# Where the largest scores of a softmax round are split, turned and read back: an attention and feed-forward kernel on one Trainium2 core

## The chip, the cores and the metric

The kernel runs on one core of one Trainium2 chip. The metric is the device time of one execution in microseconds (us); lower is better. The kernel before was timed three times: 3776.87, 3777.06 and 3780.1 us, median 3777.06 us.

A core has five engines with an instruction queue each: TensorE (PE in the profile; PEld is its loading of weights), VectorE (DVE), ScalarE (ACT), GpSimd (POOL) and SyncE (SP), which in this kernel only issues DMAs. An engine takes its queue in order; semaphores hold an instruction until what it reads is written and what it overwrites has been read.

## The reference

`x` is 4096 tokens by 256. What is computed, cut to what matters:

```python
def attention(x):
    proj = quant4(x) @ ternary_weight(Wqkv_w).T + Wqkv_b
    q = proj.reshape(B, N, h, dk).transpose(0, 2, 1, 3)     # h = 16 heads, dk = 16
    k = v = proj.reshape(B, h, N, dk)
    q, k = rotary(q), rotary(k)
    att = einsum(q @ U, k @ U) / sqrt(dk)                   # 16 x 4096 x 4096
    return quant4(softmax(att) @ v) @ ternary_weight(Wo_w).T

x = layernorm(x + attention(x))
h = silu(tlin(x, w1, s1)) * tlin(x, w2, s2)                 # 256 -> 1024
h = gelu(tlin(h, h1, hs1)); h = gelu(tlin(h, h2, hs2))      # 1024 -> 1024
out = layernorm(x + tlin(h, w3, s3))                        # 1024 -> 256
```

The softmax needs the largest score of each of the 16 x 4096 rows before the exponentials. The feed-forward weights are whole numbers; the kernel tests that on the chip, since rounded weights give the same product only then.

## The kernel before

**Tiling.** The heads go in eight pairs, the queries in eight blocks of 512. One (pair, block) is a round `u`, so there are 64 rounds, and each has 32 steps; step `s = 32 u + i`. A step does two things for two different rounds:

- `largest(s)` for round `u`: two matmuls (one for each head of the pair, `ps`, L468) give 128 queries by 512 keys of scores in a PSUM bank each, and VectorE takes the largest of each row (`mx`, L476). The `ps` buffers come from a pool of three banks (`ps_1`), two are used by each step, and other short work (L361 to L400, L439, L553) takes a bank of the same pool.
- `weights(s - 40)` for the round before or the one before that (`LAG` is 40 steps): four matmuls (L511) put scores minus the row's largest score into `sc`, a pool of two buffers, so that `sc` of step `s` waits for the exponential of step `s - 2`; ScalarE takes the exponential (`pr`, L519). The first two of the four matmuls subtract the largest scores: they multiply a matrix of -1 by `m_rows`.

Every second step `values` (L533) multiplies eight blocks of exponentials with the values. An odd step issues `largest` first and then `weights`, an even step the other way round (L700 to L705). So TensorE's order over an odd and an even step is: scores for the largest of the odd step, `weights` of the odd step, `weights` of the even step, scores for the largest of the even step, values. In what follows such a pair of steps is called a period, and it is measured from the start of an odd step's L468 matmuls to the next odd step's. A round is 16 periods.

**The largest scores of a round.** At the end of `largest` of step 31, VectorE does four short instructions in a row: it joins the partial maxima (`m`, L481), rounds them to a high part (L485), takes the remainder as a low part (L486), and turns blocks of 32 x 32 (`m_turned`, L489). SyncE writes `m_turned` to DRAM (L494) and reads it back as four rows (L499, four DMAs of 16 pieces of 128 bytes): high and low part of both heads, 512 queries in a row. That is `m_rows`, first used at step 8 of the next round (40 steps after the round began).

**Test of the weights.** In the even rounds 8 to 50, at step 14, `check_weights` loads one of 22 pieces of weights (128 x 1024) through SyncE (L589), and GpSimd rounds it and takes the difference (L593, L594). At step 30, `largest_difference` lets VectorE reduce the absolute differences of the piece to one column of `differ` (L597). At step 0 of round 52 `set_flag` makes a flag from it, by which the feed-forward part is chosen.

**Other work in the rounds.** ScalarE copies finished values at step 11 (L548), turned queries at step 26 (L446) and, in the rounds 3 to 6, 11 to 14 and so on, pieces of the next pair's keys (L362, L376, L400); VectorE forms the low part of the keys (L377) after ScalarE's L376. At step 0 of the rounds 4, 12, 20 and so on the first L376 falls on the boundary between two rounds. GpSimd rotates the next queries (L329 to L334, L431, L432), from step 6 of each round.

**What sets the order.** The program is written out under a manual schedule: `at(step, f)` files `f` in `todo[step]`, and the loop at L696 runs the list of a step ahead of that step's `largest` and `weights`. Each engine gets its instructions in that order. Within a list, what was filed first is first.

After the 64 rounds the feed-forward part (L708 on) takes the last part of the span; the change does not touch it.

Of the kernel before, what the change touches and what calls it, by code (L numbers as in the profile page):

```python
# [9 lines left out]
F32 = mybir.dt.float32  # L10
# [3 lines left out]
AF = mybir.ActivationFunctionType  # L14
ALU = mybir.AluOpType
AX = mybir.AxisListType
PSUM = bass.MemoryType.PSUM

P = 128
# [7 lines left out]
NQB = N // QB  # L27
NKT = N // P
DH = 1024
NC = DH // P  # L30
BT = 4
# [6 lines left out]
def attn_ffn_kernel(  # L38
# [22 lines left out]
    nc = tc.nc  # L61
# [4 lines left out]
    stat = ctx.enter_context(tc.tile_pool(name="stat", bufs=4))  # L66
# [13 lines left out]
    dram = ctx.enter_context(tc.tile_pool(name="dram", bufs=1, space=bass.MemoryType.DRAM))  # L80
# [157 lines left out]
    with ExitStack() as actx:  # L238
# [16 lines left out]
        m_parts = big.tile([P, 2, 2, 2, BT], F32R, name="m_parts")  # L255
        m_turned = big.tile([P, 32], F32, name="m_turned")
        m_rows = [big.tile([P, QB], F32R, name=f"m_rows{i}") for i in range(2)]
        m_dram = [dram.tile([P, 32], F32, name=f"m_dram{i}") for i in range(2)]

        qpool = actx.enter_context(tc.tile_pool(name="qpool", bufs=2))  # L260
        ppool = actx.enter_context(tc.tile_pool(name="ppool", bufs=8))
# [194 lines left out]
        def at(step, f):  # L456
            todo.setdefault(step, []).append(f)

        def largest(s):

            u, i = divmod(s, NKT)
            qt, ck = divmod(i, NKT // BT)
            if i == 0:
                mxs[u] = stat.tile([P, BT, 2, NKT // BT], F32, name="mx")
            ps = [ps_1.tile([P, 512], F32, name="ps1") for j in range(2)]
            for j in range(2):
                rows = slice(64 * j, 64 * j + 64)
                nc.tensor.matmul(  # L468
                    ps[j],
                    lhsT=qTs[u][rows, ts(qt, P)],  # L470
                    rhs=kTs[u // NQB][rows, ts(ck, 512)],
                    start=True,
                    stop=True,
                )
            for j in range(2):
                nc.vector.tensor_reduce(  # L476
                    mxs[u][:, qt, j, ck : ck + 1], ps[j], AX.X, ALU.max
                )
            if i == NKT - 1:
                m = stat.tile([P, 2, BT], F32, name="m")  # L480
                nc.vector.tensor_reduce(  # L481
                    m, mxs.pop(u).rearrange("p t j c -> p j t c"), AX.X, ALU.max
                )
                parts = m_parts[:, 0]
                nc.vector.tensor_copy(parts[:, :, 0, :], m)  # L485
                nc.vector.tensor_tensor(  # L486
                    parts[:, :, 1, :], m, parts[:, :, 0, :].bitcast(F32), ALU.subtract
                )
                nc.vector.transpose(  # L489
                    m_turned, m_parts.bitcast(F32).rearrange("p a j k t -> p (a j k t)")  # L490
                )

                turned = m_dram[u % 2]
                nc.sync.dma_start(out=turned, in_=m_turned)  # L494
                turned = turned.rearrange("(b a j k t) c -> a j k t b c", b=4, a=2, j=2, k=2)
                for j in range(2):
                    for k in range(2):
                        row = m_rows[u % 2][64 * j + k : 64 * j + k + 1, :].bitcast(F32)
                        nc.sync.dma_start(  # L499
                            out=row.rearrange("o (t b c) -> o t b c", t=BT, b=4),  # L500
                            in_=turned[0, j, k].unsqueeze(0),
                        )

        def weights(s):

# [70 lines left out]
                in_=yu.rearrange("p t j e -> p t (j e)"),  # L576
            )

        differ = stat.tile([P, 32], F32, name="differ", bufs=1)
        nc.gpsimd.memset(differ, 0.0)  # L580

        chunks = [
# [10 lines left out]
            nc.gpsimd.tensor_copy(r, w)  # L593
            nc.gpsimd.tensor_tensor(w, w, r.bitcast(F32), ALU.subtract)  # L594

        def largest_difference(i):
            nc.vector.tensor_reduce(  # L597
                differ[:, i : i + 1], wchunks.pop(i), AX.X, ALU.max, apply_absolute_value=True
            )

        def set_flag():

# [8 lines left out]
        with tc.manual_schedule():  # L611
            wchunks = {}
            for i in range(len(chunks)):
                at(NKT * (NQB + 2 * i) + 14, lambda i=i: check_weights(i))
                at(NKT * (NQB + 2 * i) + 30, lambda i=i: largest_difference(i))
            at(NKT * (NQB + 2 * len(chunks)), set_flag)
            later = set_up()
            for f in projection_steps(0, nc.vector):
                f()
            kTs[0] = kpool.tile([P, N], F32R, name="kT")  # L620
            steps = key_steps(0, kTs[0], nc.vector)
            for f in steps[:8]:
                f()
            for i, f in enumerate(steps[8:]):
                at(max(i - 1, 0), f)
            at(NQB, later)
            for b in range(1, NQB):
                steps = projection_steps(b, nc.gpsimd)
                first = NKT * (b - 2) + 16 if b > 1 else 0
                if b > 1:  # L630
                    at(
                        max(first - 20, 0),
                        lambda b=b: nc.sync.dma_start(out=x_bufs[b % 2], in_=x_t[:, ts(b, BT), :]),
                    )
                for f, step in zip(steps, (1, 1, 11, 14, 16) if b > 1 else (0, 0, 10, 13, 15)):
                    at(first + step, f)

            def load_scales():
                for name, src in (("s1", s1), ("s2", s2), ("hs1", hs1), ("hs2", hs2), ("s3", s3)):
                    nc.sync.dma_start(out=scales[name], in_=src)  # L640

            at(NKT * NQB, load_scales)
            for u in range(NU):
                pair, qb = divmod(u, NQB)
                if qb == 2 and pair + 1 < H // 2:
                    def start_keys(pair=pair, u=u):
                        kTs[pair + 1] = kpool.tile([P, N], F32R, name="kT")
                        steps = key_steps(pair + 1, kTs[pair + 1])
                        for i, f in enumerate(steps):
                            at(NKT * u + 40 + 6 * i, f)  # L650
                    at(NKT * u + 8, start_keys)

                def start_queries(u=u, pair=pair, qb=qb):
                    qTs[u] = qpool.tile([P, QB], F32R, name="qT", bufs=3)
                    natural, transposed = query_steps(pair, qb, qTs[u])
                    natural()
                    at(NKT * (u - 1) + 26 if u else 0, transposed)

                if u:
                    at(NKT * (u - 1) + (18 if u == 1 else 6), start_queries)  # L660
                else:
                    start_queries()
                base = NKT * u + LAG
                for kt in range(0, NKT, 2):
                    at(base + kt + 1 + AVLAG, lambda s=NKT * u + kt: values(s))
                at(base + NKT + AVLAG - 1, lambda u=u: finish(u, 0))
                at(base + NKT + AVLAG + 3, lambda u=u: finish(u, 1))
            last = NKT * NU
            at(last - 240, lambda: load_weights(w1_sb, w1T, 0))
            w2_sb, h1_sb, h2_sb = [None, None], [None, None], [None, None]  # L670

            def load_w2(k):
                w2_sb[k] = kprep.tile([P, 1, DH], F32R, name=f"w2_{k}", tag=("kr", "krT")[k])
                load_weights(w2_sb[k], w2T, k)

            for k in range(2):
                at(last - 230 + 10 * k, lambda k=k: load_w2(k))

            def load_h1(i):
                if i:  # L680
                    h1_sb[1] = kprep.tile([P, NC // 2, DH], F32R, name="h1b", tag="kn")
                else:
                    h1_sb[0] = kpool.tile([P, NC // 2, DH], F32R, name="h1a", tag="kT")
                load_weights(h1_sb[i], h1T, i * NC // 2)

            for i in range(2):
                at(last - 180 + 40 * i, lambda i=i: load_h1(i))
                at(last - 90, lambda i=i: load_x(i))

            def start_front():  # L690
                steps = front_steps(0, lambda shape, dt: ps_1.tile(shape, dt, name="ps1"))
                for i, f in zip((0, 6, 10, 12, 16, 18, 20), steps):
                    at(last + 2 + i, f)

            at(last - 60, start_front)
            for s in range(NKT * NU + LAG + AVLAG + 6):  # L696
                while todo.get(s):
                    todo[s].pop(0)()

                if s < NKT * NU and s % 2:  # L700
                    largest(s)
                if 0 <= s - LAG < NKT * NU:
                    weights(s - LAG)
                if s < NKT * NU and not s % 2:
                    largest(s)  # L705
# [213 lines left out]
```

## Time and profile before

| | us |
|---|---|
| median of three timed runs | 3777.06 |
| the profiled execution, its own time | 3776.26 |
| its span in the profile | 3774.5 |
| TensorE busy, of the span | 3693.2 |
| VectorE busy | 3081.1 |
| ScalarE busy | 2351.2 |
| GpSimd busy | 458.9 |
| weight loads of TensorE that waited for VectorE's `mx` (L476), 956 times | 707.3 |
| ScalarE waiting for TensorE's `sc` (L511) ahead of the exponential, 1032 times | 900.0 |
| TensorE's loads for `sc` waiting for ScalarE's exponential, 32 times | 22.8 |

The page gives the busy time of each engine, the chain of work that ended last, and groups of instructions by line with the mean time of one and what ended the idle time ahead of them. The timeline gives instructions in order of time, neighbours of one kind merged: start, duration of the whole group, engine, line, output and input, and how many; a bracket holds the idle time ahead of it and what ended it. A busy TensorE is not a TensorE at its peak, since the ends of matmuls are modelled. Times in the timeline count from the start of the span.

### The profile page before, as it was taken

To read this page: it belongs to the slowest core of one execution; us is meant where nothing else is said; L and a number is where in the kernel's file an instruction comes from. 1 tells how busy PE (TensorE), PEld (TensorE's weight loads), DVE (VectorE), ACT (ScalarE), POOL (GpSimd) and SP (SyncE) were. 2 spreads that over 40 slices of the span, in tenths; PEclk is the share of its full clock that TensorE was granted. 3 is DMA by queue.
4 is the path that set the end of the run, shared out by engine and by line. 5 is a ranking of instruction groups with operands and counts; after the bars stand their busy time and mean duration, and the time that the engine had idled before them with its cause. 6 is when DMAs were issued, how large, how long until landed. Compare 5 with 4: busy or idle time off the path is not lost.

```text
span 3774.5 us, 61722 instructions
## 1 busy us (share of the span) xinstructions
PE 3693.2 (98%) x24651; PEld 2084.5 (55%) x24651; DVE 3081.1 (82%) x5404; ACT 2351.2 (62%) x2630; POOL 458.9 (12%) x776
## 2 busy tenths in 40 slices
PE   6999999999999999999999999999999999999998
PEld 3444545555555555545455555555555548888887
DVE  6988998899889988998899889988999945555544
ACT  1566767776776767767766776767777773333333
POOL 3342011002101110011001100110010000000000
PEclk6999999999999999999999999999999999999999
DMA  1000000000000000000000000000010020000000
GB/s 36 13 14 3 9 9 9 9 9 9 9 9 9 9 9 9 9 9 9 9 9 9 8 9 9 9 3 25 3 47 14 9 70 6 17 17 23 28 6 12
DMA packets 83448, 50.92 MB, mean 13 GB/s; under 512 B 58320, under 2 KB 78032, under 8 KB 83152
## 3 DMA queue, kind: packets, MB, share of 16 engines
q1 hardware_dynamic: 79328, 35.36, 3.6%
q0 software_dynamic: 3824, 11.54, 0.9%
q8 instruction: 195, 3.19, 0.4%
q14 instruction: 101, 0.83, 0.1%
HBM read 37.44 MB, written 9.44 MB: 12 GB/s over the span
## 4 chain that ended last, share of the span: by engine, by line
PE 89%; DVE 10%; issue 1%; ACT 0%; POOL 0%; DMA 0%; SPq 0%; ACTq 0%; DVEq 0%
PE av L533 25%; PE sc L511 22%; PE ps L468 20%; PE ps_mm L751 17%; DVE mx L476 7%; PE ps L553 1%; PE ps L393 1%; PE ps L439 1%; DVE differ L597 1%; PE ps L367 0%; DVE m L481 0%; DVE m_turned L489 0%; DVE m_parts L485 0%; DVE m_parts L486 0%; PE ps L361 0%
## 5 line engine op out<-in xcount | busy, mean ns | idle before, releaser
L476 DVE TENSOR_REDUCE mx<-ps 128x1 f32<-128x512 f32 x4096 | 2552.0, 683 | 279.6 <-PE ps L468 261.0
L519 ACT ACTIVATE pr<-sc 128x1024 f32<-128x1024 f32 x2048 | 2004.2, 1023 | 902.0 <-PE sc L511 900.0
L468 PEld LDWEIGHTS ps<-kT,qT 64*128 64x128 f32 x4096 | 574.0, 185 | 1020.2 <-DVE mx L476 707.3
L468 PE MATMUL ps<-kT,qT 64*128 64x512 f32 x4096 | 1101.2, 471 | 27.4 <-DVE mx L476 23.1
L533 PE MATMUL av<-pr,v_all 128*32 128x512 f32 x8192 | 1091.4, 605 | 0.0
L511 PE MATMUL sc<-m_rows,minus 64*128 64x512 f32 x4096 | 865.0, 403 | 3.1 <-ACT pr L519 3.0
L511 PE MATMUL sc<-qT,kT 64*128 64x512 f32 x4096 | 836.1, 390 | 0.0
L511 PEld LDWEIGHTS sc<-qT,kT 64*128 64x128 f32 x4096 | 418.6, 185 | 80.2
L511 PEld LDWEIGHTS sc<-m_rows,minus 64*128 64x128 f32 x4096 | 412.3, 185 | 75.8 <-ACT pr L519 22.8
L533 PEld LDWEIGHTS av<-pr,v_all 128*32 128x32 f32 x8192 | 161.6, 108 | 258.6 <-issue 257.5
L784 ACT ACTIVATE gate<-ps_mm,sc_hs 128x512 f32<-128x512 f32 x128 | 88.2, 689 | 312.6 <-PE ps_mm L751 269.5
L733 DVE CAST h<-gate 128x512 fp32r<-128x512 f32 x128 | 54.4, 425 | 223.0 <-ACT gate L784 223.0
L593 POOL CAST wround<-xs 128x1024 fp32r<-128x1024 f32 x22 | 22.8, 1038 | 1115.5 <-DMA xs<-in_h1T 394.9
L735 DVE TENSOR_TENSOR h<-gate,h 128x512 fp32r<-128x512 f32 x192 | 132.4, 689 | 5.1
L751 PE MATMUL ps_mm<-h,h1a 128*128 128x512 f32 x512 | 128.9, 394 | 0.0
L751 PE MATMUL ps_mm<-h,h2a 128*128 128x512 f32 x512 | 127.1, 390 | 0.0
L751 PE MATMUL ps_mm<-h,h2b 128*128 128x512 f32 x512 | 126.5, 389 | 0.0
L751 PE MATMUL ps_mm<-h,h1b 128*128 128x512 f32 x512 | 126.5, 389 | 0.0
L431 POOL CAST qq<-qn 128x256 fp32r<-128x256 f32 x64 | 25.5, 398 | 739.2 <-PE ps L439 737.1
L776 DVE SCALAR_TENSOR_TENSOR gate<-ps_mm,sc_s,gate 128x512 f32<-128x512 f32 x64 | 48.0, 751 | 81.9 <-ACT gate L774 58.0
L751 PEld LDWEIGHTS ps_mm<-h,h1b 128*128 128x128 f32 x512 | 96.1, 188 | 20.1
L751 PEld LDWEIGHTS ps_mm<-h,h2b 128*128 128x128 f32 x512 | 96.1, 188 | 20.0
(147 smaller groups left out, 1963.7 us busy)
## 6 DMA issues: line engine op xcount, KB each, us to landing
xs<-in_x SPq DMA_DIRECT2D x16, 512.0 KB
m_rows<-m_dram SPq DMA_DIRECT2D x256, 2.0 KB
y_dram<-yu SPq DMA_DIRECT2D x64, 64.0 KB
xs<-in_h1T SPq DMA_DIRECT2D x8, 512.0 KB
xs<-in_h2T SPq DMA_DIRECT2D x8, 512.0 KB
yb<-y_dram SPq DMA_DIRECT2D x8, 512.0 KB
out<-xs SPq DMA_DIRECT2D x8, 512.0 KB
h1a<-in_h1T POOLq DMA_DIRECT2D x2, 1024.0 KB, 6.2
```

The costliest lines, as they stand in the source:

```text
L393: nc.tensor.matmul(ps[:, ts(k, P)], lhsT=flat[:, ts(4 * i + k, P)], rhs=identr, start=True, stop=True,)
L439: nc.tensor.matmul(ps[:, ts(t, P)], lhsT=qq[:, t].rearrange("p j k e -> p (j k e)"), rhs=identr, start=True, stop=True,)
L468: nc.tensor.matmul(ps[j], lhsT=qTs[u][rows, ts(qt, P)], rhs=kTs[u // NQB][rows, ts(ck, 512)], start=True, stop=True,)
L476: nc.vector.tensor_reduce(mxs[u][:, qt, j, ck : ck + 1], ps[j], AX.X, ALU.max)
L511: nc.tensor.matmul(ps[:, j, :], lhsT=minus[rows, :] if first else kTs[u // NQB][rows, ts(kt, P)], rhs=m_rows[u % 2][rows, :] if first else ...
L519: nc.scalar.activation(pr, ps, AF.Exp)
L533: nc.tensor.matmul(avs[u][strip : strip + 32, :], lhsT=v_all[:, 2 * (2 * pair + j) + a, c * (DK + 1) : c * (DK + 1) + 32], rhs=probs[s + k ...
L733: eng(dst[:, k, 0, :], g)
L735: nc.vector.tensor_tensor(dst[:, k, 1, :], g, dst[:, k, 0, :].bitcast(F32), ALU.subtract)
L751: nc.tensor.matmul(ps, lhsT=sb[:, ks, ts(o, P)] if split else wo[:, k, :], rhs=src[:, k, i, :], start=(k == 0 and i == 0), stop=(k == n - ...
L776: nc.vector.scalar_tensor_tensor(g, pb, scales["s2"][:, o : o + 1], gate, ALU.mult, ALU.mult)
L784: nc.scalar.activation(g, ps, AF.Gelu, scale=scales[sc][:, o : o + 1])
```

## The change

1. The high part (L485) is made by ScalarE and the low part (L486) by GpSimd, both still filed at the end of `largest` of step 31, ahead of that step's `weights`. VectorE keeps `m` (L481).
2. The turning of blocks and the DMAs move into `largest_rows(u)`, filed at step 2 of the next round.
3. `m_dram` is laid out as 32 rows of 128. One DMA writes it, as before; two DMAs read it back, each two rows of 512 values that lie together in DRAM.
4. The differences of a piece of weights are summed by ScalarE, as absolute values with an accumulated output, in two halves of 512 columns at steps 26 and 30, in place of VectorE's one reduction of 1024 columns at step 30. `differ` has 64 columns, of which 44 are written.

```diff
-        m_dram = [dram.tile([P, 32], F32, name=f"m_dram{i}") for i in range(2)]
+        m_dram = [dram.tile([32, P], F32, name=f"m_dram{i}") for i in range(2)]
...
                 parts = m_parts[:, 0]
-                nc.vector.tensor_copy(parts[:, :, 0, :], m)
-                nc.vector.tensor_tensor(
+                nc.scalar.copy(parts[:, :, 0, :], m)
+                nc.gpsimd.tensor_tensor(
                     parts[:, :, 1, :], m, parts[:, :, 0, :].bitcast(F32), ALU.subtract
                 )
-                nc.vector.transpose(
-                    m_turned, m_parts.bitcast(F32).rearrange("p a j k t -> p (a j k t)")
-                )
-
-                turned = m_dram[u % 2]
-                nc.sync.dma_start(out=turned, in_=m_turned)
-                turned = turned.rearrange("(b a j k t) c -> a j k t b c", b=4, a=2, j=2, k=2)
-                for j in range(2):
-                    for k in range(2):
-                        row = m_rows[u % 2][64 * j + k : 64 * j + k + 1, :].bitcast(F32)
-                        nc.sync.dma_start(
-                            out=row.rearrange("o (t b c) -> o t b c", t=BT, b=4),
-                            in_=turned[0, j, k].unsqueeze(0),
-                        )
+
+        def largest_rows(u):
+
+            nc.vector.transpose(
+                m_turned, m_parts.bitcast(F32).rearrange("p a j k t -> p (a j k t)")
+            )
+
+            rows = m_dram[u % 2]
+            nc.sync.dma_start(out=rows.rearrange("r (b c) -> b r c", b=4), in_=m_turned)
+            rows = rows[: 4 * BT].rearrange("(j k t) c -> j k (t c)", j=2, k=2)
+            for j in range(2):
+                nc.sync.dma_start(
+                    out=m_rows[u % 2][64 * j : 64 * j + 2, :].bitcast(F32), in_=rows[j]
+                )
...
-        differ = stat.tile([P, 32], F32, name="differ", bufs=1)
+        differ = big.tile([P, 64], F32, name="differ")
...
-        def largest_difference(i):
-            nc.vector.tensor_reduce(
-                differ[:, i : i + 1], wchunks.pop(i), AX.X, ALU.max, apply_absolute_value=True
-            )
+        def difference(i, half):
+            w = wchunks[i][:, ts(half, DH // 2)]
+            nc.scalar.activation(w, w, AF.Abs, accum_out=differ[:, 2 * i + half : 2 * i + half + 1])
...
-                at(NKT * (NQB + 2 * i) + 30, lambda i=i: largest_difference(i))
+                for half in range(2):
+                    at(NKT * (NQB + 2 * i) + 26 + 4 * half, lambda i=i, h=half: difference(i, h))
...
+                at(NKT * (u + 1) + 2, lambda u=u: largest_rows(u))
```

## The prediction

> **What bounds the kernel now.** I read the chain of waits first, then the groups of instructions, then the timeline across the end of a round.
>
> ```profile
> PE 89%; DVE 10%; issue 1%; ACT 0%; POOL 0%; DMA 0%; SPq 0%; ACTq 0%; DVEq 0%
> ```
>
> ```profile
> L597 DVE TENSOR_REDUCE differ<-xs 128x1 f32<-128x1024 f32 x22 | 26.6, 1209 | 0.0
> L481 DVE TENSOR_REDUCE m<-mx 128x8 f32<-128x64 f32 x64 | 14.1, 220 | 2.2
> L489 DVE STREAM_TRANSPOSE m_turned<-m_parts 128x32 f32<-128x32 f32 x64 | 13.6, 212 | 2.2
> L485 DVE CAST m_parts<-m 128x8 fp32r<-128x8 f32 x64 | 11.0, 172 | 2.3
> L486 DVE TENSOR_TENSOR m_parts<-m,m_parts 128x8 fp32r<-128x8 f32 x64 | 10.7, 168 | 2.2
> ```
>
> The chain is TensorE's but for 10% of VectorE's; ScalarE is on it nowhere. The end of round 59, which has no weight test (from the timeline, other lines left out):
>
> ```profile
> 2858.66 0.50 PE L468 MATMUL ps<-kT,qT 64*128 64x512 f32 x2
> ...
> 2861.37 0.50 PE L468 MATMUL ps<-kT,qT 64*128 64x512 f32 x2
> ...
> 2862.43 1.94 ACT L519 ACTIVATE pr<-sc 128x1024 f32<-128x1024 f32 x2 [0.75 <-PE sc L511]
> ...
> 2863.23 0.22 DVE L481 TENSOR_REDUCE m<-mx 128x8 f32<-128x64 f32 x1
> 2863.48 0.17 DVE L485 CAST m_parts<-m 128x8 fp32r<-128x8 f32 x1
> 2863.69 0.17 DVE L486 TENSOR_TENSOR m_parts<-m,m_parts 128x8 fp32r<-128x8 f32 x1
> 2863.89 0.21 DVE L489 STREAM_TRANSPOSE m_turned<-m_parts 128x32 f32<-128x32 f32 x1
> ...
> 2864.08 0.50 PE L468 MATMUL ps<-kT,qT 64*128 64x512 f32 x1
> ...
> 2864.73 0.50 PE L468 MATMUL ps<-kT,qT 64*128 64x512 f32 x1 [0.15 <-DVE mx L476]
> ...
> 2865.79 1.94 ACT L519 ACTIVATE pr<-sc 128x1024 f32<-128x1024 f32 x2 [1.42 <-PE sc L511]
> ...
> 2867.35 0.50 PE L468 MATMUL ps<-kT,qT 64*128 64x512 f32 x2
> ```
>
> Measure from one pair of odd-step L468 to the next: 2.71 and 2.71, then 3.27 across the boundary. 2.70 is TensorE's own pace: VectorE's four reductions of a period take 2.48 and it idles 0.22. At the boundary its four short instructions cost it some 0.8, of which 0.22 is idle anyway, and TensorE loses 0.57: the second score matmul has no bank. The end of round 48, which has the test:
>
> ```profile
> 2350.12 1.21 DVE L597 TENSOR_REDUCE differ<-xs 128x1 f32<-128x1024 f32 x1
> ...
> 2351.09 0.49 PE L468 MATMUL ps<-kT,qT 64*128 64x512 f32 x1
> ...
> 2354.60 0.50 PE L468 MATMUL ps<-kT,qT 64*128 64x512 f32 x1
> ...
> 2357.88 0.50 PE L468 MATMUL ps<-kT,qT 64*128 64x512 f32 x2
> ```
>
> 3.51, then 3.28: the test costs a further 0.81. So VectorE's extra work at the boundary is on the path, 0.57 or 1.38 each time. The question is what stands there next.
>
> [...] L446 (512) takes 582 ns, and two exponentials of 1.02 take 1.94. [...] here L95's Abs and the exponentials after it share one table load, so the new Abs adds none. [...] the trace has ScalarE's L446 and L376 always run between the exponentials they are filed between.
>
> **The change, part by part.**
>
> *VectorE.* It loses L485 and L486 (0.17 each) at each boundary and L597 (1.21) 22 times. `m` stays, 0.22. L489, 0.21, moves two steps on, a period later, where another 0.22 is idle. So VectorE alone would hold TensorE no longer: worth the 0.57 and 0.81 above.
>
> *ScalarE's copy.* The wait is the point. The copy is filed ahead of step 31's exponential, waits for `m`, and the exponentials of steps 31 and 32 are queued behind it; TensorE's `sc` of steps 33 and 34 waits for these, since `sc` has two buffers. On round 59's clock:
> - `m` ends at 2863.45. Copy starts 0.08 later (0.03 is what L377 shows between engines; 0.05 more because the copy waits for two semaphores): 2863.53. Bounds 0.03 and 0.08.
> - [...] Less the overlap of 0.09 the exponential starts at 2863.63, not 2862.43.
> - Two exponentials: 2865.57. Near the end of the attention, where exponentials bound, TensorE restarts 0.05 after one ends and its second pair of `sc` matmuls comes 0.33 later: 2865.95.
> - Undisturbed, that second pair would come 1.03 after the L468 of 2864.08 (as in the following periods): 2865.11. TensorE loses 0.84.
>
> So the stall of 0.57 goes and one of 0.84 stands there. Everything else in that period hides under it: `m`, L489 (if the cover went, at most 0.21 x 63 = 13 us), and VectorE's lateness.
>
> *The halves of the test.* Each 512 columns: 0.63 (L95), less 0.09. At step 26, ahead of L446: it puts the exponential 0.54 later, which then ends when TensorE would come for its buffer; cost 0 (0.1 to 0.3 if the accumulator adds as much). At step 30 it delays `sc` of step 32 by 0.2, which lies ahead of the stall of 0.84 and is swallowed. GpSimd's difference is done in the first third of the round, so no wait.
>
> *GpSimd and SyncE.* L486 on GpSimd: 8 elements, about 0.21 from L332 (64: 0.326) and L432 (256: 0.733); done near 2864.0, and VectorE turns near 2865.9. Behind it in GpSimd's queue are query rotations, not needed for some 20 steps. SyncE's write moves 2.0 later; nothing is filed between. Before, it was issued at 2864.13, the reads from 2865.61, four of 0.66; first use near 2873.6. Now write 2866.2, two reads done issuing near 2868.9, landed near 2870.4 if a read takes the write's 1.48: 3 us to spare. No gain from fewer reads, no cost.
>
> *The sum* over the 63 boundaries with a follower, before against after:
> - 23 plain ones (6, 7, 9 and so on): 0.57 to 0.84, +6.2
> - 17 with the test: 1.38 to 0.84, -9.2
> - 5 with the test and a key piece (L400) at step 30, which stretches the period: 0.71 to 0.84, +0.6
> - 7 with a key piece at step 34 (5, 13, ...): 1.31 to about 1.15, since the piece's 0.66 of TensorE lies partly under the wait, -1.1
> - 7 with L376 at step 32 (3, 11, ...): L376 is behind the delayed exponential and VectorE's L377 waits for it ahead of all reductions. In round 19 L377 began at 998.12; it can begin after copy, exponential and L376, at about 999.17: +1.05 each, +7.4
> - 4 early ones (0, 1, 2, 4), where projection work shares the stall: -0.35 each, -1.4
>
> Sum +2.5 on the profiled execution's 3776.26 (span 3774.5 and 1.8 around it): 3778.8; the median lies 0.8 above it. I say 3779. Feed-forward part: unchanged.
>
> **The rivals.**
>
> *ScalarE absorbs the wait (faster).* It idles 0.75 in each period and 902 us in all, and two `sc` buffers give slack. Then all boundary stalls go: 0.57 x 23 + 1.38 x 17 + 0.71 x 5 + 0.57 x 7 + 1.4 = 46: 3731. Against it: the wait for `m` is 1.2, the slack of the even exponential is only about 0.3 (it ends 0.3 ahead of the next weight load for its buffer). Chance 0.13.
>
> *ScalarE's copy is dearer (slower).* If it takes 0.29 and overlaps with nothing, the exponentials start 0.20 later still, at all 52 boundaries of the first, second, third and fifth kind: +10.4, so 3790. It is slower by more than 0.2% from about 0.1 above my price. For it: L194, the only tiny ScalarE instruction here, takes 292 ns[...]. Accumulation in the halves would add to it. Chance 0.28.
>
> *The rows come late (slower).* If the write over new pieces or the reads take 3 us more, `sc` of step 40 waits in every round, 63 us for each us beyond. The 4 us of slack now speak against it. Chance 0.04.
>
> *The change takes nothing off VectorE.* The instruction order says it does: L485, L486 and L597 are gone from its queue.
>
> **How the numbers follow.** The forecast's case has 0.55. A measurement tells about 0.2% (7.5 us) from no change. The forecast's own spread is some 8 us: 0.1 per boundary either way is 6, the L376 boundaries are uncertain by 4. Faster: 0.13 and a little of the forecast's case, 0.16. Slower: 0.04, two thirds of the dearer copy's 0.28, and part of the forecast's case, 0.34. Same: 0.50. The range from 3764 to 3798 holds the forecast and the dearer copy with its bounds and leaves out the absorbed wait and late rows, 0.17.
>
> **What would show it.** In a plain boundary: ScalarE's copy near 0.08 after `m` ends, with a long idle time ahead of it that `m` ends; the two exponentials right behind; the weight load of `sc` at step 34 waiting for L519; a period of about 3.5 where 3.27 stood; 3.5 then 2.7, not 3.51 then 3.28, in test rounds. In the chain of waits ScalarE gets a share, VectorE's falls. Waits of `sc` for `pr` rise from 22.8 us to 40 or more. I am wrong if the period is below 3.0 (the wait is absorbed), if L376 boundaries are no longer than before, or if `sc` waits for the rows' DMA.

## The result and the profile after

The median is 3770.24 us (14 runs, 3769.45 to 3770.6) against 3778.39 for the kernel before beside it (14 runs, 3776.87 to 3780.16): ratio 0.9978, interval 0.997 to 0.9986. That is 8.1 us faster, where 3779 and no measurable change were forecast. The profiled execution took 3770.6 with a span of 3768.8 (before: 3776.26 and 3774.5). Of all the runs below one, of e5 (4844.6 us), fell in a slow state, with a granted TensorE clock of 0.65, and is left out.

The chain of waits after, and the line of the waits that the forecast named (waiting engine and tile, whom it waited for: total us, times, longest):

```profile
PE 89%; DVE 6%; ACT 3%; issue 1%; POOL 0%; DMA 0%; ACTq 0%; SPq 0%
```

```profile
PEld sc L511 <- ACT pr L519: 84.8, 173, 3.5
```

VectorE's share of the chain fell from 10% to 6%, ScalarE's rose from 0% to 3%, and TensorE waited for the exponentials 84.8 us in place of 22.8. TensorE is still what the chain mostly runs through; the boundary has changed hands. The groups that answer to those of before:

```profile
L599 ACT ACTIVATE xs<-xs 128x512 f32<-128x512 f32 x44 | 27.3, 620 | 0.0
L481 DVE TENSOR_REDUCE m<-mx 128x8 f32<-128x64 f32 x64 | 14.1, 220 | 2.2
L486 POOL TENSOR_TENSOR m_parts<-m,m_parts 128x8 fp32r<-128x8 f32 x64 | 13.2, 206 | 2233.4 <-ACT m_parts L485 2233.4
L492 DVE STREAM_TRANSPOSE m_turned<-m_parts 128x32 f32<-128x32 f32 x64 | 12.9, 202 | 0.6 <-POOL m_parts L486 0.6
L485 ACT CAST m_parts<-m 128x8 fp32r<-128x8 f32 x64 | 12.6, 197 | 112.8 <-DVE m L481 112.8
L599 ACT ACTIVATION_READ_ACCUMULATOR xs<-xs 128x1 f32 x44 | 8.5, 193 | 0.0
```

The copy itself costs 12.6 us in all; waiting for `m` cost ScalarE 112.8, which is 1.76 each time. GpSimd's 2233.4 us of idle time ahead of L486 cost nothing: it had nothing to do. The last line stood in the forecast only as a possible extra of 0.1 to 0.3: each half brings a second instruction, 193 ns, that reads the accumulator. It and the sum overlap by 0.10. The sums brought no table load: there are 36 in the whole span, before and after.

The end of round 59 again, which has no test (timeline of the changed kernel, other lines left out):

```profile
2852.57 0.50 PE L468 MATMUL ps<-kT,qT 64*128 64x512 f32 x2
...
2854.43 0.22 DVE L481 TENSOR_REDUCE m<-mx 128x8 f32<-128x64 f32 x1
...
2854.74 0.20 ACT L485 CAST m_parts<-m 128x8 fp32r<-128x8 f32 x1 [1.86 <-DVE m L481]
2854.84 3.85 ACT L519 ACTIVATE pr<-sc 128x1024 f32<-128x1024 f32 x4
2855.02 0.20 POOL L486 TENSOR_TENSOR m_parts<-m,m_parts 128x8 fp32r<-128x8 f32 x1 [40.59 <-ACT m_parts L485]
...
2855.28 0.52 PE L468 MATMUL ps<-kT,qT 64*128 64x512 f32 x2
...
2855.91 0.19 PEld L511 LDWEIGHTS sc<-m_rows,minus 64*128 64x128 f32 x2 [0.43 <-ACT pr L519]
...
2856.82 0.19 PEld L511 LDWEIGHTS sc<-m_rows,minus 64*128 64x128 f32 x2 [0.61 <-ACT pr L519]
...
2857.02 0.20 DVE L492 STREAM_TRANSPOSE m_turned<-m_parts 128x32 f32<-128x32 f32 x1
...
2858.72 0.49 PE L468 MATMUL ps<-kT,qT 64*128 64x512 f32 x2
```

From odd-step L468 to the next: 2.71, then 3.44 where 3.27 stood. Four exponentials in one block of 3.85 without a gap show that ScalarE is late and catching up; both loads of `sc` wait for one. The scores of step 31 were complete at 2853.53, but their exponential starts at 2854.84: it is behind the copy in ScalarE's queue. The end of round 48, which has the test:

```profile
2342.67 0.62 ACT L599 ACTIVATE xs<-xs 128x512 f32<-128x512 f32 x1
2343.19 0.19 ACT L599 ACTIVATION_READ_ACCUMULATOR xs<-xs 128x1 f32 x1
2343.28 1.02 ACT L519 ACTIVATE pr<-sc 128x1024 f32<-128x1024 f32 x1
2343.38 0.50 PE L468 MATMUL ps<-kT,qT 64*128 64x512 f32 x2
...
2345.49 0.20 ACT L485 CAST m_parts<-m 128x8 fp32r<-128x8 f32 x1 [1.19 <-DVE m L481]
...
2346.24 0.50 PE L468 MATMUL ps<-kT,qT 64*128 64x512 f32 x2
...
2349.47 0.50 PE L468 MATMUL ps<-kT,qT 64*128 64x512 f32 x2
```

2.86 and 3.23, where 3.51 and 3.28 stood (the forecast had 3.5 and 2.7): the test has left the boundary, and ScalarE's wait has come in its place. The end of round 19, with a key piece at step 32:

```profile
992.64 0.20 ACT L485 CAST m_parts<-m 128x8 fp32r<-128x8 f32 x1 [1.87 <-DVE m L481]
...
993.00 1.03 ACT L519 ACTIVATE pr<-sc 128x1024 f32<-128x1024 f32 x1 [0.17 <-ACT m_parts L485]
993.92 0.58 ACT L376 CAST kn<-ps 128x512 fp32r<-128x512 f32 x1
994.54 0.69 DVE L377 TENSOR_TENSOR kn<-ps,kn 128x512 fp32r<-128x512 f32 x1 [1.99 <-ACT kn L376]
```

VectorE now stands still for 1.99 until L376 is done, ahead of all its reductions. Round 19 is the dearer form: here the exponential starts 0.36 after the copy starts, and 0.10 after it in round 59.

From the trace of each kernel I took what a boundary loses beyond two undisturbed periods (2.707, but 2.586 in e4), as a mean over the boundaries of a kind, in us:

| boundaries (number) | before | after | e1 | e2 | e3 | e4 | e5 | e6 | e7 |
|---|---|---|---|---|---|---|---|---|---|
| plain (23) | 0.57 | 0.73 | -0.01 | 0.34 | 0.56 | 0.00 | -0.01 | 0.34 | 0.96 |
| test (17) | 1.37 | 0.68 | 0.15 | 0.34 | 0.56 | 0.21 | -0.01 | 1.15 | 0.90 |
| test and key piece at step 30 (5) | 0.71 | 0.67 | -0.01 | 0.34 | 0.57 | -0.01 | -0.01 | 0.48 | 0.90 |
| key piece at step 34 (7) | 1.43 | 1.14 | 0.80 | 1.22 | 1.44 | 0.91 | 0.81 | 1.22 | 1.33 |
| L376 at step 32 (7) | 1.73 | 2.42 | 1.51 | 1.69 | 1.75 | 1.60 | 1.51 | 1.67 | 2.58 |
| early (4) | 1.26 | 0.63 | 0.62 | 1.05 | 1.26 | 0.54 | 0.62 | 1.04 | 0.80 |

### The profile page after: what moved, and what is told of

The parts are those of the page before. It is cut to its first block, busy times and chain, and to the rows that moved or that the text cites. A ratio compares the mean times of both kernels' runs of the same rounds, so it can differ in the third digit from the quotient of the medians.

```text
span 3768.8 us, 61593 instructions
## 1 busy us (share of the span) xinstructions
PE 3688.5 (98%) x24651; PEld 2065.1 (55%) x24651; DVE 3041.0 (81%) x5254; ACT 2381.5 (63%) x2782; POOL 471.5 (13%) x840
## 4 chain that ended last, share of the span: by engine, by line
PE 89%; DVE 6%; ACT 3%; issue 1%; POOL 0%; DMA 0%; ACTq 0%; SPq 0%
PE av L533 25%; PE sc L511 23%; PE ps L468 19%; PE ps_mm L753 17%; DVE mx L476 5%; ACT pr L519 2%; PE ps L553 1%; PE ps L393 1%; PE ps L439 1%; DVE m L481 0%; PE ps L367 0%; PE ps L361 0%; PE ps L147 0%; DVE ma L119 0%; PE ps_mm L798 0%
## 5 line engine op out<-in xcount | busy, mean ns | idle before, releaser
L476 DVE TENSOR_REDUCE mx<-ps 128x1 f32<-128x512 f32 x4096 | 2564.2, 684 | 308.4 <-PE ps L468 280.2
L519 ACT ACTIVATE pr<-sc 128x1024 f32<-128x1024 f32 x2048 | 2003.9, 1023 | 755.4 <-PE sc L511 743.7
L533 PE MATMUL av<-pr,v_all 128*32 128x512 f32 x8192 | 1092.0, 605 | 0.0
L468 PEld LDWEIGHTS ps<-kT,qT 64*128 64x128 f32 x4096 | 549.1, 185 | 972.1 <-DVE mx L476 699.1
L468 PE MATMUL ps<-kT,qT 64*128 64x512 f32 x4096 | 1047.7, 470 | 14.0 <-DVE mx L476 7.9
L511 PE MATMUL sc<-m_rows,minus 64*128 64x512 f32 x4096 | 851.6, 409 | 16.2 <-ACT pr L519 12.2
L511 PE MATMUL sc<-qT,kT 64*128 64x512 f32 x4096 | 815.0, 391 | 0.0
L511 PEld LDWEIGHTS sc<-m_rows,minus 64*128 64x128 f32 x4096 | 392.5, 185 | 134.4 <-ACT pr L519 84.8
L511 PEld LDWEIGHTS sc<-qT,kT 64*128 64x128 f32 x4096 | 393.2, 185 | 74.1
L533 PEld LDWEIGHTS av<-pr,v_all 128*32 128x32 f32 x8192 | 161.6, 108 | 267.9 <-issue 266.7
L486 POOL TENSOR_TENSOR m_parts<-m,m_parts 128x8 fp32r<-128x8 f32 x64 | 13.2, 206 | 2233.4 <-ACT m_parts L485 2233.4
L753 PEld LDWEIGHTS ps_mm<-h,h2a 128*128 128x128 f32 x512 | 95.6, 188 | 19.6
```

The costliest lines, as they stand in the source:

```text
L468: nc.tensor.matmul(ps[j], lhsT=qTs[u][rows, ts(qt, P)], rhs=kTs[u // NQB][rows, ts(ck, 512)], start=True, stop=True,)
L476: nc.vector.tensor_reduce(mxs[u][:, qt, j, ck : ck + 1], ps[j], AX.X, ALU.max)
L511: nc.tensor.matmul(ps[:, j, :], lhsT=minus[rows, :] if first else kTs[u // NQB][rows, ts(kt, P)], rhs=m_rows[u % 2][rows, :] if first else ...
L519: nc.scalar.activation(pr, ps, AF.Exp)
L533: nc.tensor.matmul(avs[u][strip : strip + 32, :], lhsT=v_all[:, 2 * (2 * pair + j) + a, c * (DK + 1) : c * (DK + 1) + 32], rhs=probs[s + k ...
L753: nc.tensor.matmul(ps, lhsT=sb[:, ks, ts(o, P)] if split else wo[:, k, :], rhs=src[:, k, i, :], start=(k == 0 and i == 0), stop=(k == n - ...
```

## The experiments

What they test is the forecast's own mechanism with sizes mended: taking work off VectorE is worth its stalls, and the copy's place in ScalarE's queue gives most of it back. The theories are numbered anew in each expectation. Each kernel was timed beside the kernel before, whose median was 3777.75 us for e1 to e4 and 3777.31 for e5 to e7, against 3778.39 beside the changed kernel; so a difference from the changed kernel is uncertain by about 1 us. The code cuts are shortened; a `...` stands for what is left out.

**e6, the turn alone.** The kernel before, with L489 and the DMAs moved into `largest_rows`, step 2 of the next round, two reads; the parts and the test stay on VectorE.

```diff
+        def largest_rows(u):
+            nc.vector.transpose(m_turned, ...)
+            # one write, two reads, as in the changed kernel
...
+                at(NKT * (u + 1) + 2, lambda u=u: largest_rows(u))
```

> The kernel before, with only the turn of blocks and its DMAs moved to step 2 of the next round and the two reads in place of four; high and low part stay on VectorE, the weight test too. If the moved turn is worth what it was worth beside the halves (plain boundaries 0.57 to 0.34): 63 x 0.2, 11 to 13 us less than before, near 3766 us. If the turn's gain is only there because something else had made room, or the later rows hold the exponentials' scores: 3775 us or above.

3764.25 us, 0.9962 (0.9948 to 0.9976). That is 13.1 below its kernel before, where the first of the two expectations had 11 to 13. A plain boundary went from 0.57 to 0.34: the turn's 0.21 was on the path, and two steps later it is off it. The later turn and the rows' later return cost nothing. The run does not tell the move from the two reads in place of four; neither here nor in the kernel before does a step wait for the rows.

**e3, the halves alone.** The kernel before, with the test's sums on ScalarE.

```diff
-                at(NKT * (NQB + 2 * i) + 30, lambda i=i: largest_difference(i))
+                for half in range(2):
+                    at(NKT * (NQB + 2 * i) + 26 + 4 * half, lambda i=i, h=half: difference(i, h))
```

> The kernel before, with only the weight differences moved to ScalarE in halves at steps 26 and 30. Theory 1 (the gain of the change is this part alone, and the moved parts lose): boundaries with the test go from 1.38 to about 0.65, plain ones stay at 0.57: 17 x 0.7 = 12 us less than before, near 3766 us, less than the changed kernel. Theory 2 (the parts moved off VectorE gain as well): between the kernel before and the changed kernel, 3771 to 3778 us.

3761.78 us, 0.996 (0.9947 to 0.9974). That is 16.0 below its kernel before. Test boundaries now lose what plain ones do, 0.56: all of the 0.81 of each test is regained, in spite of the extra reads of the accumulator. The run is below the changed kernel, as theory 1 has it, but this part isn't the whole gain: the turn has its own (e6).

**e2, both, with the parts on VectorE.** The changed kernel with two engines put back:

```diff
-                nc.scalar.copy(parts[:, :, 0, :], m)
-                nc.gpsimd.tensor_tensor(
+                nc.vector.tensor_copy(parts[:, :, 0, :], m)
+                nc.vector.tensor_tensor(
```

> The changed kernel, with the high and the low part made by VectorE again at the end of step 31; turn, two reads and the halves on ScalarE stay as changed. Theory 1 (ScalarE's wait costs 0.74 at a plain boundary, VectorE's three short instructions 0.6 of which 0.23 is idle): plain boundaries 0.37, those with the test about 0.45, those with L376 about 1.3; 23 x 0.37 + 22 x 0.2 + 7 x 1 = some 20 us less than the changed kernel, near 3750 us. Theory 2 (VectorE is what binds, and taking the two instructions off it was the gain): 43 to 63 x 0.3 us more than the changed kernel, 3785 us or above.

3750.23 us, 0.993 (0.9916 to 0.9943). It is 27.5 below its kernel before, about the sum of e3 (16.0) and e6 (13.1), and 20 below the changed kernel. So giving the two parts to ScalarE and GpSimd where the change puts them costs 20 us on balance, although it takes 0.34 of work off VectorE each time. This is the part of the change that lost. That the time met the expected 3750 is in part luck: test boundaries came out at 0.34 in place of 0.45, those with L376 at 1.69 in place of 1.3.

**e1, the same parts two steps later.** The changed kernel, with the copy and the remainder filed at step 33, one step ahead of the turn, in place of the end of step 31.

```diff
-                parts = m_parts[:, 0]
-                nc.scalar.copy(...)
-                nc.gpsimd.tensor_tensor(...)
+        def largest_parts(u):
...
+            nc.scalar.copy(...)
+            nc.gpsimd.tensor_tensor(...)
...
+                at(NKT * (u + 1) + 1, lambda u=u: largest_parts(u))
```

> The changed kernel, with ScalarE's copy (high part) and GpSimd's remainder (low part) filed at step 33 ahead of that step's exponential, in place of the end of step 31; all else the same. Theory 1, the wait behind ScalarE's copy is what holds TensorE at the boundary: the copy falls into ScalarE's idle 0.75 us of that period, and m (ended 1 us before) holds nobody. Plain boundaries go from 0.74 us to 0.05 or less, those with the weight test from 0.68 to about 0.15 (what the second half of the test costs), those with L376 at step 32 from 2.4 to about 1.3. Sum 23 x 0.7 + 22 x 0.53 + 7 x 1.1 + 7 x 0.4: about 38 us less than the changed kernel, near 3732 us. Theory 2, the boundary's loss is VectorE's own (m, and the turn of blocks in the next period): no change, 3770 us.

3731.57 us, 0.9876 (0.986 to 0.9891). Same instructions, same engines; 38.7 us below the changed kernel by the queue position alone. The end of round 59 in its timeline (L491 is the copy here, L498 the turn, L525 the exponential):

```profile
2816.95 0.50 PE L468 MATMUL ps<-kT,qT 64*128 64x512 f32 x2
...
2818.03 1.94 ACT L525 ACTIVATE pr<-sc 128x1024 f32<-128x1024 f32 x2 [0.78 <-PE sc L517]
...
2818.82 0.22 DVE L481 TENSOR_REDUCE m<-mx 128x8 f32<-128x64 f32 x1
...
2819.66 0.52 PE L468 MATMUL ps<-kT,qT 64*128 64x512 f32 x2
...
2819.86 0.20 ACT L491 CAST m_parts<-m 128x8 fp32r<-128x8 f32 x1
...
2820.75 1.94 ACT L525 ACTIVATE pr<-sc 128x1024 f32<-128x1024 f32 x2 [0.69 <-PE sc L517]
...
2821.40 0.20 DVE L498 STREAM_TRANSPOSE m_turned<-m_parts 128x32 f32<-128x32 f32 x1
...
2822.36 0.50 PE L468 MATMUL ps<-kT,qT 64*128 64x512 f32 x2
```

2.71 and 2.70: nothing of this boundary is left, while those with L376 at step 32 still lose 1.51. The copy has no bracket, since `m` was ready long before ScalarE came to it, and the exponentials on either side wait for TensorE, not TensorE for them. The time of the forecast's faster rival, 3731, is what the change gives when the copy is not waited for.

**e5, the halves at odd steps as well.** e1 and one further edit, aimed at the 0.15 that e1 still loses in test rounds:

```diff
-                    at(NKT * (NQB + 2 * i) + 26 + 4 * half, ...)
+                    at(NKT * (NQB + 2 * i) + 27 + 2 * half, ...)
```

> The kernel with the parts at step 33, and the halves of the weight test at the odd steps 27 and 29 in place of 26 and 30. An odd step's exponential follows ScalarE's idle 0.75 us, in which a half (0.62 and 0.19 for reading the accumulator, overlapping) mostly fits. If the 0.15 us left at boundaries with the test come from the half at step 30 pushing that step's exponential: they go, 17 x 0.15 = 2.6 us less, near 3729 us. If a half costs TensorE wherever it stands: 3732 us as with the halves at 26 and 30, or more, since two odd periods are now hit.

3728.17 us (median of three) against 3777.31, 0.9866 (0.9848 to 0.9884). Test boundaries went from 0.15 to nothing: the half at step 30 was what delayed the even step's exponential, and ahead of an odd step's there is room. It is the fastest of the kernels that search all scores, though its interval and e1's overlap; the table shows the difference more clearly than the times.

**e7, the copy twice.** To price the copy itself, the disputed term of the forecast's slower rival:

```diff
                 nc.scalar.copy(parts[:, :, 0, :], m)
+                nc.scalar.copy(parts[:, :, 0, :], m)
```

> The changed kernel with ScalarE's copy of the high part made twice at the end of step 31. Theory 1 (what counts is when ScalarE is free for the exponential of step 31): each of the 52 boundaries that follow the copy's price is later by 0.1 to 0.25, so 5 to 13 us more than the changed kernel, 3776 to 3783 us. Theory 2 (the wait for m counts, not the copy's length, and there is slack behind it): 3770 us.

3783.33 us, 1.0014 (1.0007 to 1.0021): 13 above the changed kernel, at the upper end of the 5 to 13 that theory 1 had. The end of round 59 in its timeline (L520 is the exponential here):

```profile
2866.89 0.20 ACT L485 CAST m_parts<-m 128x8 fp32r<-128x8 f32 x1 [1.87 <-DVE m L481]
2867.11 0.20 ACT L486 CAST m_parts<-m 128x8 fp32r<-128x8 f32 x1
2867.22 3.79 ACT L520 ACTIVATE pr<-sc 128x1024 f32<-128x1024 f32 x4
2867.43 0.52 PE L468 MATMUL ps<-kT,qT 64*128 64x512 f32 x2
...
2871.09 0.50 PE L468 MATMUL ps<-kT,qT 64*128 64x512 f32 x2
```

The second copy, which writes the same tile, starts 0.22 after the first, so all of it is added; the exponentials start 0.11 after it starts, much as they do after one copy (0.10). A plain boundary loses 0.96 in place of 0.73, 0.23 more. So what delays ScalarE here delays TensorE by as much, and a copy dearer by 0.2 would have made the change slower than before by 0.14%: the rival's price was right, its premise wrong.

**e4, half of each reduction.** The kernel before, with the largest taken over half of the columns, to see what a period takes when VectorE is never late.

```diff
-                    mxs[u][:, qt, j, ck : ck + 1], ps[j], AX.X, ALU.max
+                    mxs[u][:, qt, j, ck : ck + 1], ps[j][:, :256], AX.X, ALU.max
```

> The kernel before, with each reduction to the largest score over 256 of the 512 columns; it leaves out half of the scores in the search for the largest, everything else is as it was. It asks what TensorE's own pace in an undisturbed period is. Theory 1 (in each period the second score matmul of the even step still waits about 0.1 us for a bank that VectorE's reduction holds, which is what TensorE got back after the wait in the changed kernel): undisturbed periods of 2.60 us, the stalls at boundaries gone, some 160 us less than before. Theory 2 (2.70 is TensorE's own pace): periods stay at 2.70, only boundary stalls go, 40 to 70 us less.

3607.95 us, a single run without an interval. The end of round 59 in its timeline:

```profile
2703.22 0.50 PE L468 MATMUL ps<-kT,qT 64*128 64x512 f32 x2
...
2704.25 0.18 PEld L468 LDWEIGHTS ps<-kT,qT 64*128 64x128 f32 x2
2704.48 0.40 PE L468 MATMUL ps<-kT,qT 64*128 64x512 f32 x2
...
2704.80 1.07 PE L533 MATMUL av<-pr,v_all 128*32 128x512 f32 x8
...
2705.80 0.50 PE L468 MATMUL ps<-kT,qT 64*128 64x512 f32 x2
```

A period is 2.58, across a plain boundary too, as theory 1 had it (2.60); test boundaries still lose 0.21. The even step's two weight loads run together in 0.18; in the changed kernel, away from the boundary, they are spread over 0.41:

```profile
2850.92 0.41 PEld L468 LDWEIGHTS ps<-kT,qT 64*128 64x128 f32 x2
...
2851.15 0.50 PE L468 MATMUL ps<-kT,qT 64*128 64x512 f32 x2
...
2851.58 1.06 PE L533 MATMUL av<-pr,v_all 128*32 128x512 f32 x8
```

So there the second load waits for a bank that VectorE still reads. No bracket shows it, since the timeline merges the pair, but the times of the single loads and of the semaphore that VectorE's reductions (L476) raise do: in all 611 periods of the changed kernel that lie within 0.008 of 2.707 (580 before) the second load starts 0.04 us after such an update, and 0.24 after the first load in the median. In e4 the two start 0.003 apart in the median, with the update already there. The undisturbed 2.707 therefore holds 0.12 of waiting for VectorE (2.707 less 2.586).

## Why the forecast went wrong

The mechanism was the one that the runs show, and so were the places; the sizes in the sum were off by 11 us together, enough to turn +2.5 into a gain of 8.5. (The 3779 is also 0.6 less than the forecast's own terms give, 3778.8 and 0.8.) In us over the boundaries of a kind, forecast and measured (number times the difference of the first two columns above, rounding apart):

| kind | forecast | measured |
|---|---|---|
| plain (23) | +6.2 | +3.7 |
| test (17) | -9.2 | -11.8 |
| test and key piece at step 30 (5) | +0.6 | -0.2 |
| key piece at step 34 (7) | -1.1 | -2.0 |
| L376 at step 32 (7) | +7.4 | +4.8 |
| early (4) | -1.4 | -2.5 |
| all other periods of the attention | 0 | -0.5 |
| sum | +2.5 | -8.5 |
| start, and from the end of round 63 on | 0 | +2.8 |

The last two lines make the span's change, -5.7; the medians differ by 8.1, since the profiled execution of before lay 2.1 below its 14-run median and that of after 0.4 above.

**The failed step is the 0.84 of "TensorE loses 0.84".** Its first half held to the hundredth. The copy starts 0.09 after `m` ends and takes 0.197, the exponential behind it overlaps it by 0.09 (0.094 in the median), and so it starts 0.19 after `m` ends, where the forecast has 0.18 (2863.63 less 2863.45). The second pair of score matmuls of the delayed step comes 4.59 after the L468 of step 31 (2857.16 less 2852.57), where the forecast put 4.58 (2865.95 less 2861.37):

```profile
2857.16 0.39 PE L511 MATMUL sc<-qT,kT 64*128 64x512 f32 x2
2857.16 0.19 PEld L468 LDWEIGHTS ps<-kT,qT 64*128 64x128 f32 x2
...
2857.39 0.40 PE L468 MATMUL ps<-kT,qT 64*128 64x512 f32 x2
...
2857.72 1.07 PE L533 MATMUL av<-pr,v_all 128*32 128x512 f32 x8
```

But the step took "2.70 is TensorE's own pace" as the measure of what follows, and 0.12 of that is waiting for VectorE's banks. While TensorE is stopped by ScalarE, VectorE frees the banks, and the even step's L468 runs at once: its two loads take 0.19 where an undisturbed period has 0.41, and the values (L533) follow its matmuls 0.33 later (2857.72 less 2857.39), as in e4 (0.32), where an undisturbed period has 0.43. That is the 0.11. So a stall from ScalarE takes the place of one from VectorE that the forecast counted as work: 0.73, not 0.84. Over the 45 boundaries of the first three kinds that is 5 us of the 11.

**Two waits taken for granted.** The copy was to wait for two semaphores each time. It does in 42 rounds and has one to wait for in the 22 with the test. The instruction that holds the additional wait, from the source view of L485:

```profile
L485 ACTq EVENT_SEMAPHORE  x42: 17/17/17, 96.9 to 3035.7; - x42
```

With it the copy starts 0.089 after `m` ends, without it 0.034. So a test boundary loses 0.68, not 0.73, and 22 of them together 1.2 us less. Why the test's rounds need only the one is not shown.

**Stalls added where they overlap.** L376 cost 1.05 more in rounds 11, 27, 35 and 43 (1.30 to 2.35), as worked out. I put the same on rounds 3 and 51, which lost 2.32 and 3.27 already, to other work in the same place: they went to 2.34 and 2.63. Round 19 went to 2.62; the exponential there starts 0.36 after the copy in place of 0.10, and the reason stays open. With a piece at step 34, six boundaries went from 1.31 to 1.08 and round 5 from 2.11 to 1.49. The early boundaries gave 0.6 each, not 0.35, presumably for a like reason, since the projection's work stops TensorE in the same place.

**What was left out.** The boundary of round 63 has no follower in the sum, but the copy's wait there delays its exponentials too, 1.17 us; the tail lost some 1.3 to TensorE's clock (below); and the start took 0.3 more.

**What held.** VectorE's extra work is off the path: with the copy out of the way (e1) a plain boundary loses nothing, and nor does a test boundary with odd steps (e5). GpSimd's part took 0.206 (0.21 forecast). The rows are in time: e6 gains what the turn costs and no step waits for them. The halves at 26 and 30 cost nothing in this kernel, since the stall at the boundary hides the 0.15 that e1 shows. The rival of the absorbed wait fell on its place in the queue, not on ScalarE's load.

In short: turning later -13 (e6), halves -16 (e3), the two parts +20 on balance (the changed kernel against e2). Of these 20, taking them off VectorE is worth -19 (e1 against e2), and the copy's place at the end of the round costs +39 (the changed kernel against e1).

## What to carry to other kernels

A short instruction given to an idler engine can cost the queue behind it its wait as well as its length: ask what is queued behind it, and file it where its input has long been there. Here a copy of 0.2 us that waited 1.76 us for its input made the kernel 39 us slower at the end of a round than two steps later. And a steady period is not the bound's own pace until a run with the other engine out of the way has shown it (2.707 here, 2.586 in e4), since a merged pair of loads can hide a wait; a stall that frees what the period waits for costs less than that period suggests (0.73 here, not 0.84).

## What the hardware showed besides

Near the end of the attention ScalarE loads a table for L194 and one back for L519, 1.28 us each, and TensorE stands idle for 3.0 us. What follows differs from kernel to kernel. Windows of 5 us behind that gap, before, after and e1 (window, length, busy time and instructions of PE, PEld, DVE, ACT and POOL, then the granted clock, DMA share and GB/s):

```profile
3073.00:3078.00 5.00, 4.97 (x36) 1.88 (x36) 0.00 (x0) 4.18 (x5) 0.00 (x0) 1.00 0.00 0
```

```profile
3066.00:3071.00 5.00, 4.92 (x28) 1.82 (x28) 0.00 (x0) 3.77 (x5) 0.00 (x0) 0.66 0.00 0
```

```profile
3026.00:3031.00 5.00, 4.66 (x20) 1.86 (x20) 0.00 (x0) 2.55 (x4) 0.00 (x0) 0.50 0.00 0
```

The same gap has a whole clock behind it before (1.00). After, it is half (0.50) for 3.41 us, from 3067.57 to 3070.98. In e1 it is half for some 6.8, from within the gap on, by its 0.95, 0.50 and 0.87 in three windows of 5 us from 3021 on. So there are 36, 28 and 20 matmuls in the 5 us shown, of which TensorE is idle for 0.34 in e1. What decides between a whole and a half clock is not shown, since no run moved the gap by itself. In the changed kernel the third group of values (L533) behind the gap starts 6.43 after TensorE resumes, 5.15 before: the half clock cost 1.3 us.
